# A graph layer with table casts, first gathers and node ends put in another order

## The chip, the cores and the metric

The kernel runs on one NeuronCore of a Trainium2 chip. Its engines work side by side: TensorE (PE; its weight loads are shown apart as PEld), VectorE (DVE), ScalarE (ACT), GpSimd (POOL) and SyncE (SP), which here only issues transfers. The metric is the device time of one execution in microseconds; the time of a kernel is the median of its runs.

## The reference, cut to what matters

6250 nodes with 128 features, 100000 edges sorted by destination, a message network of three layers, the mean of the messages at each destination, a node network of two layers, and a layer norm of the result:

```python
row, col = src, dst                                   # 100000 edges, dst sorted
msg_in = concatenate([x[row], x[col]], axis=-1)       # 100000 x 256
h = relu(msg_in @ Wm1 + bm1)                          # 256 wide
h = relu(h @ Wm2 + bm2)                               # 256 wide
messages = h @ Wm3 + bm3                              # 128 wide
agg = segment_sum(messages, col) / clip(count, 1)
upd = relu(concatenate([x, agg]) @ Wn1 + bn1) @ Wn2 + bn2
out = layernorm(x + (x + upd))                        # 6250 x 128
```

## The kernel before, in words

**Preparation.** The first layer is split: x @ (upper half of Wm1) is table A, x @ (lower half) is table B, both written to DRAM, one row for each node. The 49 tiles of 128 nodes are worked in 13 blocks of four (`turn` transposes, `a_table` writes A, `b_table` writes B three blocks behind). A is kept in 32 bits. B is kept as three bf16 terms: a cast of the product (L249, ACT), the rest (L250, DVE), the rest's cast (L252 on POOL for the early tiles, L254 on ACT from block 9 on), and what still remains (L255, DVE); L256 stores it (SP). The `rest` tiles have two buffers, the `bt` tiles six. `x_part` computes for a block of nodes the part of the node network that needs no messages (two products of 128x512 and a bias each); blocks 0, 1, 2 are done beside the last tables, 3 to 8 behind them, 9 and 12 inside the first two steps of the edge loop, 10 and 11 at its end.

**Edge loop.** 196 groups of 512 edges. `fetch` gathers four times 128 rows of A by source (L412, an indirect transfer on POOL; it can't start before all of A is in DRAM) and loads four windows of rows of B (L418, SP; not before all of B is in DRAM). Four `ag` and four `bw` buffers. `hot` builds one-hot matrices on DVE. `first_layer` transposes the rows of A into PSUM (L449) and adds B by a one-hot product (L455); ACT applies bias and relu (L460). `second_layer` multiplies with Wm2 (L469), DVE takes a maximum (L471). `sums` adds over destinations in a window (L478), `add_up` transposes the sums (L489) and adds them into `acc` in SBUF (L494). Groups are fetched two steps ahead; in step g PE does first layer g, sums of g - 3 and second layer g - 1. The 24 memsets that clear `acc` (L376) run on POOL.

**Node stage.** `products` (third layer of the summed messages), `hidden` (first node layer), `norm` (second node layer, the sum with 2x, statistics, square root, scale and shift, store). 15 blocks of nodes: one of 106 nodes, two of 256, ten of 512 and two of 256. `norm` runs two blocks behind `hidden`. In `norm` the tiles y, mv, sd and o have two buffers each; the scaled result o is made by ACT, one instruction for each 128 nodes (L718).

**What sets the order.** PE follows the order of the program text throughout. Elsewhere a planner orders the instructions by its own estimate of when they are ready, except inside stretches marked as manual, where an engine follows the text: DVE and ACT from the blocks 3 to 8 of `x_part` to the sixth step of the edge loop, and at the end of the edge loop. Each engine works its instructions in one queue, in order; SP's transfers, stores of A and B and loads of rows of B, share one queue too.

Of the kernel before, what the change touches and what calls it, by code (L numbers as in the profile page):

```python
# [9 lines left out]
F32 = mybir.dt.float32  # L10
# [3 lines left out]
ALU = mybir.AluOpType  # L14
# [5 lines left out]
P = 128  # L20
# [7 lines left out]
def kernel(  # L28
# [122 lines left out]
    with tc.tile_pool(name="prep", bufs=1) as prep, tc.tile_pool(  # L151
# [73 lines left out]
        INDICES = 6  # L225
        LATE = BLOCKS - 4
        xu = xT, x_sb.rearrange("p t d -> p (t d)")
# [16 lines left out]
        def b_table(t0):  # L244
            m = min(2, NT - t0)
            pbt = products(t0, m, 1)
            bt = brow.tile([P, 2 * 3 * H], BF16, name="bt").rearrange("p (t c h) -> p t c h", t=2, c=3)
            rest = brow.tile([P, 2, H], F32, name="rest", bufs=2)
            nc.scalar.copy(bt[:, :m, 0], pbt[:, :m])  # L249
            nc.vector.tensor_sub(rest[:, :m], pbt[:, :m], bt[:, :m, 0])  # L250
            if t0 < 4 * LATE:
                nc.gpsimd.tensor_copy(bt[:, :m, 1], rest[:, :m])  # L252
            else:
                nc.scalar.copy(bt[:, :m, 1], rest[:, :m])  # L254
            nc.vector.tensor_sub(bt[:, :m, 2], rest[:, :m], bt[:, :m, 1])  # L255
            nc.sync.dma_start(btab[t0 * P:(t0 + m) * P].rearrange("(t p) c h -> p t c h", p=P), bt[:, :m])  # L256
# [74 lines left out]

        X_BESIDE, X_BEHIND, X_FIRST, X_END = [0, 1, 2], [3, 4, 5, 6, 7, 8], [9, 12], [10, 11]
        assert sorted(X_BESIDE + X_BEHIND + X_FIRST + X_END) == list(range(BLOCKS))

        turn(0)
        for i in range(BLOCKS + BEHIND):
# [9 lines left out]
            if i >= BEHIND:  # L346
                for t0 in range(4 * (i - BEHIND), min(4 * (i - BEHIND) + 4, NT), 2):
                    b_table(t0)
            if BLOCKS - 1 <= i < BLOCKS - 1 + len(X_BESIDE):
                whole(x_part(X_BESIDE[i - BLOCKS + 1], bank_pb, (nc.scalar, nc.scalar)))  # L350
# [15 lines left out]

        turns = ExitStack()
        turns.enter_context(tc.manual_schedule(engines={ENG.DVE, ENG.Activation}))
        for b in X_BEHIND:
            whole(x_part(b, bank_pb, (nc.scalar, nc.vector)))  # L370


        PIECE = NPAD // 8
        for c in range(HC + 1):
            for k in range(8):
                nc.gpsimd.memset(acc[:, c, k * PIECE:(k + 1) * PIECE], 0.0)  # L376

# [17 lines left out]
    with edge, tc.tile_pool(name="wk", bufs=2) as wk, tc.tile_pool(  # L395
# [10 lines left out]

        def fetch(idx, nt, firsts):


            ag = ld.tile([P, GT, H], F32, name="ag", bufs=4)  # L410
            for j in range(GT):
                nc.gpsimd.indirect_dma_start(  # L412
                    out=ag[:, j, :], out_offset=None, in_=atab[:, :],
                    in_offset=bass.IndirectOffsetOnAxis(ap=idx[:, j:j + 1], axis=0))
            bw = ld.tile([P, 2, H], BF16, name="bw", bufs=4)
# [116 lines left out]
        for i in range(NG + ahead + 1):  # L532
# [11 lines left out]
            if i < NG:  # L544
# [4 lines left out]
                elif i % 2 == 0:  # L549
                    dbs = early.pop(0) if early else destinations(i, min(2, NGF - i), dst_row)  # L550
                st[i] = dict(nt=nt, got=fetch(srcT[:, i, :], nt, firsts), db=dbs.pop(0))
            g = i - ahead
# [17 lines left out]
            if 0 <= g < NG:  # L570
                s = st[g]
                s["h1"] = first_layer(ag, bw, oht, s["nt"])
                if first:

                    make_hot(g + 1)
                    whole(x_part(first.pop(0), bank_p2, (nc.scalar, nc.vector)))
            k = g - lag
            if 0 <= k < NG:
                s = st[k]
                s["part"] = sums(s["oh"], s["h2"], s["nt"])  # L580
            m = g - 1
            if 0 <= m < NG:
                s = st[m]
# [61 lines left out]
    with tc.tile_pool(name="nd", bufs=2) as nd, tc.tile_pool(name="nr", bufs=1) as nr, tc.tile_pool(  # L645
# [43 lines left out]

        def norm(b, u):  # L690
            n0, n1 = nodes_of[b]
# [9 lines left out]
            nc.sync.dma_start(x2[:r, :k], x2tab[n0:n1, :].rearrange("(t p) d -> p t d", p=r))  # L701
            y = nd.tile([P, 4, D], F32, name="y")
            nc.vector.tensor_add(y[:r, :k, :], x2[:r, :k, :], pot[:r, :k, :])  # L703
            st = nd.tile([P, 4, 6], F32, name="st")
            mv = nd.tile([P, 4, 2], F32, name="mv")
            for i in range(k):
                nc.vector.bn_stats(st[:r, i, :], y[:r, i, :])
                nc.vector.bn_aggr(mv[:r, i, :], st[:r, i, :])
            sd = nd.tile([P, 4], F32, name="sd")
            nc.scalar.activation(sd[:r, :k], mv[:r, :k, 1], AF.Sqrt, bias=eps[:r])  # L710
            rs = nd.tile([P, 4], F32, name="rs")
            nc.vector.reciprocal(rs[:r, :k], sd[:r, :k])  # L712
            sh = nd.tile([P, 4], F32, name="sh")
            nc.vector.scalar_tensor_tensor(sh[:r, :k], mv[:r, :k, 0], -1.0, rs[:r, :k],  # L714
                                           op0=ALU.mult, op1=ALU.mult)
            o = nd.tile([P, 4, D], F32, name="o")
            for i in range(k):
                nc.scalar.activation(o[:r, i, :], y[:r, i, :], AF.Identity, bias=sh[:r, i:i + 1],  # L718
                                     scale=rs[:r, i:i + 1])
            if r == P:  # L720
# [7 lines left out]
        us = {}  # L728
        for b in range(B + BACK):
            if b < B:  # L730
                us[b] = hidden(b, aggs.pop(b))
            if b >= BACK:
                norm(b - BACK, us.pop(b - BACK))
            if b + FORE < B:
                aggs[b + FORE] = products(b + FORE)


# [27 lines left out]
```

## Time and profile before

| What | us |
|---|---|
| median of 4 runs | 1210.07 (1208.21 to 1212.18) |
| profiled execution, its own time | 1207.48 |
| its span, first to last instruction | 1205.7 |
| PE busy | 1176.4 |
| POOL busy | 804.4, of which 784 gathers 752.6 |
| DVE, ACT busy | 670.8, 454.8 |
| PE starts on the first group of edges | 82.89 |
| last gather ends | 1098.3 |
| node stage's first product on PE | 1130.1 |
| PE's last product ends | 1195.96 |
| ACT's last instruction ends | 1202.78 |

Times in the timelines count from the start of the span. A line of a timeline has the start, the length (from the start of the first to the end of the last of a merged run), the engine, the line of the kernel, the operation, output and inputs, the number of instructions, and in brackets how long the engine had been idle before it and what ended that. PE and the weight loads overlap, and matmuls are pipelined, so a busy PE is not a PE at its peak. The granted TensorE clock is 0.998 of full speed over the span.

### The profile page before, as it was taken

The page shows a single profiled execution, that of the slowest core. Times are in us where ns is not written, and L with a number is a line of the kernel's source. Part 1 is how long each engine was busy: PE and PEld are TensorE (multiplying, and loading weights), DVE is VectorE, ACT ScalarE, POOL GpSimd, SP SyncE. Part 2 cuts the span into 40 slices and gives each one's busy share as a digit, 9 for nine tenths or more (in the row PEclk, how much of TensorE's full clock was granted, in tenths as well). Part 3 has the DMA queues.
Part 4 walks back from the last instruction along what each step waited for, and adds up shares of the span by engine and source line. Part 5 has one row for each costly group of instructions (what it writes and reads, how often), then busy time and mean ns, then how long its engine had stood idle before and what let it go on. Part 6 is the DMA issues. An engine that isn't in the chain of part 4 may idle for free. (4 is left out here: it accounts for less than half of the span.)

```text
span 1205.7 us, 32797 instructions
## 1 busy us (share of the span) xinstructions
PE 1176.4 (98%) x11196; PEld 893.8 (74%) x11197; DVE 670.8 (56%) x2080; ACT 454.8 (38%) x1163; POOL 804.4 (67%) x859
## 2 busy tenths in 40 slices
PE   7989999999999999999999999999999999999996
PEld 6747777777777777777777777777777777777565
DVE  5863655555555555555555555555555555555586
ACT  5663333333333333333333333333333333333256
POOL 8267777777777777777777777777777777773220
PEclk9999999999999999999999999999999999999999
DMA  9886666666555555555555555555555555552333
GB/s 294 289 258 180 184 183 178 191 188 181 152 152 148 151 149 153 154 152 152 151 147 150 153 153 152 148 155 148 149 153 153 152 152 151 145 150 62 96 111 105
DMA packets 173672, 193.66 MB, mean 161 GB/s; under 512 B 30844, under 2 KB 145486, under 8 KB 173488
## 3 DMA queue, kind: packets, MB, share of 16 engines
q0 software_dynamic: 37984, 103.35, 31.1%
q1 hardware_dynamic: 106956, 61.93, 17.7%
q10 hardware_dynamic: 28564, 26.27, 8.2%
q8 instruction: 90, 1.47, 0.5%
q14 instruction: 78, 0.64, 0.2%
HBM read 168.92 MB, written 22.88 MB: 159 GB/s over the span
## 5 line engine op out<-in xcount | busy, mean ns | idle before, releaser
L412 POOL DMA_INDIRECT ag<-atab,srcT x784 | 752.6, 960 | 282.5 <-issue 184.6
L469 PE MATMUL ph<-w,h 128*128 128x256 f32 x3128 | 727.5, 386 | 1.2 <-ACT x_sb L318 1.2
L469 PEld LDWEIGHTS ph<-w,h 128*128 128x128 f32 x3128 | 578.1, 190 | 152.4 <-DVE acc L494 65.7
L460 ACT ACTIVATE h<-ph,b 128x256 f32<-128x256 f32 x782 | 307.1, 475 | 674.9 <-PE ph L455 505.4
L471 DVE TENSOR_TENSOR h<-ph,nb 128x512 f32<-128x512 f32 x391 | 270.4, 692 | 412.8 <-PE ph L469 409.0
L494 DVE TENSOR_TENSOR acc<-acc,pt 128x63 f32 x782 | 172.2, 220 | 33.5 <-PE ph L455 2.9
L449 PE MATMUL ph<-ident,ag 64*128 64x64 f32 x3128 | 129.9, 223 | 0.6 <-DVE b L382 0.6
L478 PE MATMUL pg<-h,oh 128*32 128x257 f32 x1564 | 125.6, 392 | 0.0
L449 PEld LDWEIGHTS ph<-ident,ag 64*128 64x128 f32 x3128 | 113.2, 139 | 2.1 <-ACT h L460 0.8
L433 DVE TENSOR_SCALAR oht<-db,pbase 128x128 bf16<-128x128 int32 x392 | 105.5, 344 | 1.2 <-PE ph L455 1.0
L489 PEld LDWEIGHTS pt<-ident,part 64*128 64x128 f32 x1173 | 51.1, 136 | 66.4 <-issue 65.8
L455 PE MATMUL ph<-oht,bw 64*128 64x128 bf16 x1564 | 76.8, 216 | 3.0 <-DMA bw<-btab 2.6
L489 PE MATMUL pt<-ident,part 64*128 64x64 f32 x1173 | 78.0, 238 | 0.6 <-DVE acc L494 0.4
L481 ACT COPY part<-pg 128x257 f32<-128x257 f32 x196 | 76.8, 392 | 4.0 <-PE pg L478 4.0
L436 DVE TENSOR_TENSOR oh<-iota_n,dloc 128x128 f32<-128x128 f32 x196 | 55.1, 281 | 21.3 <-PE pg L478 20.2
L676 POOL TENSOR_TENSOR agg<-total,rc 128x512 f32<-128x512 f32 (+2 forms) x15 | 16.0, 1070 | 69.1 <-DVE total L673 62.1
L455 PEld LDWEIGHTS <-bw 64*128 64x128 bf16 x1564 | 53.5, 96 | 3.8 <-DMA bw<-btab 3.2
L232 PE MATMUL pbt<-w,xT 128*128 128x256 f32 x196 | 48.1, 391 | 2.4 <-ACT bt L241 1.2
L478 PEld LDWEIGHTS pg<-h,oh 128*32 128x32 f32 x1564 | 30.8, 108 | 21.7 <-issue 0.8
L232 PEld LDWEIGHTS pbt<-w,xT 128*128 128x128 f32 x196 | 36.5, 195 | 10.7 <-ACT bt L241 2.4
L252 POOL CAST bt<-rest 128x512 bf16<-128x512 f32 x18 | 11.9, 664 | 26.3 <-DVE rest L250 17.2
L698 PEld LDWEIGHTS pot<-wu,u 128*128 128x128 f32 (+1 forms) x196 | 24.0, 191 | 5.5 <-issue 4.8
(109 smaller groups left out, 416.5 us busy)
## 6 DMA issues: line engine op xcount, KB each, us to landing
bw<-btab SPq DMA_DIRECT2D x782, 32.0 KB
db<-in_dst_dram ACTq DMA_DIRECT2D x194, 128.0 KB
ag<-atab,srcT POOLq DMA_INDIRECT x784
btab<-bt SPq DMA_DIRECT2D x24, 384.0 KB
atab<-bt SPq DMA_DIRECT2D x24, 256.0 KB
xd<-in_x_dram SPq DMA_DIRECT2D x12, 256.0 KB
x2tab<-xd SPq DMA_DIRECT2D x12, 256.0 KB
x_sb<-in_x_dram SPq DMA_DIRECT2D x5, 512.0 KB
```

The source lines that it names most:

```text
L232: nc.tensor.matmul(pbt[:, a, :], xT[:, (t0 + a) * P:(t0 + a + 1) * P], w1[:, k, :], start=True, stop=True)
L412: nc.gpsimd.indirect_dma_start(out=ag[:, j, :], out_offset=None, in_=atab[:, :], in_offset=bass.IndirectOffsetOnAxis(ap=idx[:, j:j + 1], a ...
L433: nc.vector.tensor_scalar(oht[:n, k, :], db[:n, k * P:(k + 1) * P], pb_cols[:n, k:k + 1], None, op0=ALU.is_equal)
L449: nc.tensor.matmul(phs[h][:, c, u * NQ:(u + 1) * NQ], ag[halves[h], u, c * P:(c + 1) * P], ident[halves[h], halves[h]], is_transpose=True, ...
L455: nc.tensor.matmul(phs[h][:, c, k * P:(k + 1) * P], bw[halves[h], k, c * P:(c + 1) * P], oht[halves[h], k, :], start=False, stop=True, ski ...
L460: nc.scalar.activation(h1[:, c, h * 2 * P:(h + 1) * 2 * P], phs[h][:, c, :], AF.Relu, bias=b1[:, c:c + 1])
L469: nc.tensor.matmul(ph2[:, a, :], h1[:, c, (j0 + a) * P:(j0 + a + 1) * P], w2[:, c, :], start=(c == 0), stop=(c == HC - 1))
L471: nc.vector.tensor_tensor(h2[:, j0:j0 + 2, :H], ph2, nb2.to_broadcast([P, 2, H]), op=ALU.max)
L478: nc.tensor.matmul(pg[j * WN:(j + 1) * WN, :], oh[:, j, :], h2[:, j, :], start=True, stop=True, skip_group_check=True)
L481: nc.scalar.copy(part[:n, :], pg[:n, :])
L489: nc.tensor.matmul(pt[:, c, :], rows, ident[halves[h], halves[h]], is_transpose=True, start=True, stop=True, skip_group_check=True)
L494: nc.vector.tensor_add(window, window, pts[j // 2][:, :, k:k + WB])
```

## The change

- The second term of B is always cast on POOL; the cast on ACT for the late tiles goes.
- The memsets of `acc` come first, and from there to the sixth step of the edge loop POOL too follows the order of the text.
- The gathers of the first two columns of group 0 are put after the tables of blocks 10 and 11, so that the casts of the last blocks lie between and behind them; the other two follow in `fetch`.
- Before the gathers of groups 3, 4 and 5, DVE copies one element of the first layer's result of group 0, 1 and 2 into the `ag` tile, so that the gather can't start before that result is there.
- `x_part`: blocks 0 and 1 beside the tables, 2 to 7 behind, 8 in the first step of the loop, 9 and 12 in the second, there with the first half's bias on DVE and the second's on ACT (before: the other way round).
- Second layer 0 is done in step 0, behind block 8, not in step 1.
- `norm` is split into `moments`, `deviation` and `scaled`. y, mv, sd and o get three buffers. For the last three blocks DVE and ACT follow the text, the scaling of a block stands behind the moments of the next, and some of its 128-node pieces are done on DVE.

```diff
-            if t0 < 4 * LATE:
-                nc.gpsimd.tensor_copy(bt[:, :m, 1], rest[:, :m])
-            else:
-                nc.scalar.copy(bt[:, :m, 1], rest[:, :m])
+            nc.gpsimd.tensor_copy(bt[:, :m, 1], rest[:, :m])
...
-        X_BESIDE, X_BEHIND, X_FIRST, X_END = [0, 1, 2], [3, 4, 5, 6, 7, 8], [9, 12], [10, 11]
+        X_BESIDE, X_BEHIND, X_FIRST, X_END = [0, 1], [2, 3, 4, 5, 6, 7], [[8], [9, 12]], [10, 11]
...
+        PIECE = NPAD // 8
+        for c in range(HC + 1):
+            for k in range(8):
+                nc.gpsimd.memset(acc[:, c, k * PIECE:(k + 1) * PIECE], 0.0)
+        turns = ExitStack()
+        turns.enter_context(tc.manual_schedule(engines={ENG.Pool}))
+
+        def gather(ag, idx, js):
+            for j in js:
+                nc.gpsimd.indirect_dma_start(
+                    out=ag[:, j, :], out_offset=None, in_=atab[:, :],
+                    in_offset=bass.IndirectOffsetOnAxis(ap=idx[:, j:j + 1], axis=0))
+
+        def rows_of_a():
+            return ld.tile([P, GT, H], F32, name="ag", bufs=4)
+
+        first_rows = rows_of_a()
         turn(0)
         for i in range(BLOCKS + BEHIND):
...
             if i >= BEHIND:
                 for t0 in range(4 * (i - BEHIND), min(4 * (i - BEHIND) + 4, NT), 2):
                     b_table(t0)
+            if i - BLOCKS in (0, 1):
+                gather(first_rows, srcT[:, 0, :], [i - BLOCKS])
             if BLOCKS - 1 <= i < BLOCKS - 1 + len(X_BESIDE):
                 whole(x_part(X_BESIDE[i - BLOCKS + 1], bank_pb, (nc.scalar, nc.scalar)))
...
-        def fetch(idx, nt, firsts):
-            ag = ld.tile([P, GT, H], F32, name="ag", bufs=4)
-            for j in range(GT):
-                nc.gpsimd.indirect_dma_start(
-                    out=ag[:, j, :], out_offset=None, in_=atab[:, :],
-                    in_offset=bass.IndirectOffsetOnAxis(ap=idx[:, j:j + 1], axis=0))
+        def fetch(idx, nt, firsts, rows=None, have=(), gate=None):
+            ag = rows or rows_of_a()
+            if gate is not None:
+                nc.vector.tensor_copy(ag[0:1, 0, 0:1], gate)
+            gather(ag, idx, [j for j in range(GT) if j not in have])
...
-                st[i] = dict(nt=nt, got=fetch(srcT[:, i, :], nt, firsts), db=dbs.pop(0))
+                more = dict(rows=first_rows, have=(0, 1)) if i == 0 else {}
+                if 3 <= i <= 5:
+                    more["gate"] = st[i - 3]["h1"][0:1, 0, 0:1]
+                st[i] = dict(nt=nt, got=fetch(srcT[:, i, :], nt, firsts, **more), db=dbs.pop(0))
...
                     make_hot(g + 1)
-                    whole(x_part(first.pop(0), bank_p2, (nc.scalar, nc.vector)))
+                    for b in first.pop(0):
+                        whole(x_part(b, bank_p2, (nc.vector, nc.scalar)))
...
-            m = g - 1
-            if 0 <= m < NG:
+            m = g - 1 if g else g
+            if 0 <= m < NG and "h2" not in st[m]:
...
-            y = nd.tile([P, 4, D], F32, name="y")
+            y = nd.tile([P, 4, D], F32, name="y", bufs=3)
...
+        for b in range(B - 1):
+            us[b] = hidden(b, aggs.pop(b))
             if b >= BACK:
-                norm(b - BACK, us.pop(b - BACK))
+                y, mv = moments(b - BACK, us.pop(b - BACK))
+                scaled(b - BACK, y, mv, deviation(b - BACK, mv), [nc.scalar] * 4)
             if b + FORE < B:
                 aggs[b + FORE] = products(b + FORE)
+        with tc.manual_schedule(engines={ENG.DVE, ENG.Activation}):
+            us[B - 1] = hidden(B - 1, aggs.pop(B - 1))
+            ends = [(B - 3, [nc.scalar, nc.scalar, nc.scalar, nc.vector]), (B - 2, [nc.scalar, nc.vector]),
+                    (B - 1, [nc.vector, nc.scalar])]
+            before = None
+            for b, engines in ends:
+                y, mv = moments(b, us.pop(b))
+                sd = deviation(b, mv)
+                if before:
+                    scaled(*before)
+                before = b, y, mv, sd, engines
+            scaled(*before)
```

In `scaled` a piece on ACT is the activation as before (identity with scale and bias by node); on DVE it is a `tensor_scalar` of 128x128, multiply and add, with the same two columns.

More of the change, by code (lines that the diff above doesn't have):

```diff
@@ L225 @@
         INDICES = 6
-        LATE = BLOCKS - 4
         xu = xT, x_sb.rearrange("p t d -> p (t d)")
@@ L328, in bank_pb @@
             return pb.tile([P, 2, H], F32, name="pxu", tag="pbt")
-        X_BESIDE, X_BEHIND, X_FIRST, X_END = [0, 1, 2], [3, 4, 5, 6, 7, 8], [9, 12], [10, 11]
-        assert sorted(X_BESIDE + X_BEHIND + X_FIRST + X_END) == list(range(BLOCKS))
+        X_BESIDE, X_BEHIND, X_FIRST, X_END = [0, 1], [2, 3, 4, 5, 6, 7], [[8], [9, 12]], [10, 11]
+        assert sorted(X_BESIDE + X_BEHIND + sum(X_FIRST, []) + X_END) == list(range(BLOCKS))
+        PIECE = NPAD // 8
[12 more added lines that the diff above has]
+        first_rows = rows_of_a()
         turn(0)
@@ L365 @@
         early = [destinations(2 * k, 2, dst_row) for k in range(3)]
-        turns = ExitStack()
         turns.enter_context(tc.manual_schedule(engines={ENG.DVE, ENG.Activation}))
@@ L370 @@
             whole(x_part(b, bank_pb, (nc.scalar, nc.vector)))
[L373 to L376, printed above, removed]
         pb3 = pp.tile([P, 1], F32, name="pb3", tag="pp")
@@ L688, in hidden, with moments @@
             return u
-        def norm(b, u):
+        def moments(b, u):
             n0, n1 = nodes_of[b]
@@ L701, in norm @@
             nc.sync.dma_start(x2[:r, :k], x2tab[n0:n1, :].rearrange("(t p) d -> p t d", p=r))
-            y = nd.tile([P, 4, D], F32, name="y")
+            y = nd.tile([P, 4, D], F32, name="y", bufs=3)
             nc.vector.tensor_add(y[:r, :k, :], x2[:r, :k, :], pot[:r, :k, :])
             st = nd.tile([P, 4, 6], F32, name="st")
-            mv = nd.tile([P, 4, 2], F32, name="mv")
+            mv = nd.tile([P, 4, 2], F32, name="mv", bufs=3)
             for i in range(k):
@@ L708, in norm, with deviation, scaled @@
                 nc.vector.bn_aggr(mv[:r, i, :], st[:r, i, :])
-            sd = nd.tile([P, 4], F32, name="sd")
-            nc.scalar.activation(sd[:r, :k], mv[:r, :k, 1], AF.Sqrt, bias=eps[:r])
+            return y, mv
+        def deviation(b, mv):
+            r = min(P, nodes_of[b][1] - nodes_of[b][0])
+            k = -(-(nodes_of[b][1] - nodes_of[b][0]) // P)
+            sd = nd.tile([P, 4], F32, name="sd", bufs=3)
+            nc.scalar.activation(sd[:r, :k], mv[:r, :k, 1], AF.Sqrt, bias=eps[:r])
+            return sd
+        def scaled(b, y, mv, sd, engines):
+            n0, n1 = nodes_of[b]
+            k = -(-(n1 - n0) // P)
+            r = min(P, n1 - n0)
             rs = nd.tile([P, 4], F32, name="rs")
@@ L715, in norm @@
                                            op0=ALU.mult, op1=ALU.mult)
[L716 to L719, printed above, removed]
+            o = nd.tile([P, 4, D], F32, name="o", bufs=3)
+            for i, eng in zip(range(k), engines):
+                if eng is nc.scalar:
+                    eng.activation(o[:r, i, :], y[:r, i, :], AF.Identity, bias=sh[:r, i:i + 1], scale=rs[:r, i:i + 1])
+                else:
+                    eng.tensor_scalar(o[:r, i, :], y[:r, i, :], rs[:r, i:i + 1], sh[:r, i:i + 1],
+                                      op0=ALU.mult, op1=ALU.add)
             if r == P:
@@ L728 @@
         us = {}
-        for b in range(B + BACK):
-            if b < B:
-                us[b] = hidden(b, aggs.pop(b))
+        for b in range(B - 1):
+            us[b] = hidden(b, aggs.pop(b))
             if b >= BACK:
-                norm(b - BACK, us.pop(b - BACK))
+                y, mv = moments(b - BACK, us.pop(b - BACK))
+                scaled(b - BACK, y, mv, deviation(b - BACK, mv), [nc.scalar] * 4)
             if b + FORE < B:
                 aggs[b + FORE] = products(b + FORE)
+        assert BACK == 2
+        with tc.manual_schedule(engines={ENG.DVE, ENG.Activation}):
[10 more added lines that the diff above has]
+            scaled(*before)
 _INS = ['x', 'src', 'dst', 'L0_gnn_Wm1', 'L0_gnn_bm1', 'L0_gnn_Wm2', 'L0_gnn_bm2', 'L0_gnn_Wm3',
```

## The prediction

> **What bounds the kernel now.** I read the page first (share of each engine, the 40 slices), then the table of groups, then the waits of PE alone, and last the timelines of the only two places where PE is not full: the passage into the edge loop (60 to 105 us) and the end (1190 us on).
>
> ```profile
> PE 1176.4 (98%) x11196; PEld 893.8 (74%) x11197; DVE 670.8 (56%) x2080; ACT 454.8 (38%) x1163; POOL 804.4 (67%) x859
> PE   7989999999999999999999999999999999999996
> L412 POOL DMA_INDIRECT ag<-atab,srcT x784 | 752.6, 960 | 282.5 <-issue 184.6
> ```
>
> PE is the bound: 29 us of the 1205.7 are idle, at both ends of the span. In the loop a group repeats each 5.27 us on PE (the part transposes start at 111.09 and again at 116.36), while its four gathers take 4 x (0.96 + 0.30) = 5.04 us on POOL. So POOL follows PE by a hair, which matters for anything that starts the gathers later. The passage, on PE:
>
> ```profile
> 82.89 0.71 PE L449 MATMUL ph<-ident,ag 64*128 64x64 f32 x16 [0.57 <-DVE b L382]
> 84.76 0.23 PE L455 MATMUL ph<-oht,bw 64*128 64x128 bf16 x2 [1.07 <-DMA bw<-btab]
> 85.45 0.34 PE L455 MATMUL ph<-oht,bw 64*128 64x128 bf16 x5 [0.46 <-DMA bw<-btab]
> 89.09 0.23 PE L455 MATMUL ph<-oht,bw 64*128 64x128 bf16 x2 [0.69 <-DMA bw<-btab]
> 89.73 0.34 PE L455 MATMUL ph<-oht,bw 64*128 64x128 bf16 x5 [0.40 <-DMA bw<-btab]
> 91.92 3.72 PE L469 MATMUL ph<-w,h 128*128 128x256 f32 x16 [1.23 <-ACT x_sb L318]
> ...
> 96.44 3.72 PE L469 MATMUL ph<-w,h 128*128 128x256 f32 x16
> ```
>
> The reader is to see 4.4 us of waiting: 2.6 for rows of B, 1.2 for a PSUM bank that ScalarE frees late, 0.6 at the change of pools. Behind 96.44 PE waits 0.3 and 0.4 us once each and then not again until the node stage. The rows of B are late because table B is:
>
> ```profile
> 76.59 0.39 ACT L254 CAST bt<-rest 128x256 bf16<-128x256 f32 x1
> 77.02 0.43 DVE L255 TENSOR_TENSOR bt<-rest,bt 128x256 bf16<-128x256 f32 x1 [0.64 <-ACT bt L254]
> 77.47 0.34 SPq L256 DMA_DIRECT2D btab<-bt  x1
> 81.09 0.57 SPq L418 DMA_DIRECT2D bw<-btab  x1
> ```
>
> The last cast of B sits behind work of the node parts on ScalarE, the last store goes out at 77.47, and the first load of its rows can be issued only at 81.09, 3.6 us later. The end, on VectorE and ScalarE:
>
> ```profile
> 1194.05 0.69 DVE L703 TENSOR_TENSOR y<-x,pot 128x512 f32<-128x512 f32 x1 [0.56 <-ACT o L718]
> 1196.89 0.42 DVE L703 TENSOR_TENSOR y<-x,pot 128x256 f32<-128x256 f32 x1 [0.83 <-ACT o L718]
> 1199.47 0.42 DVE L703 TENSOR_TENSOR y<-x,pot 128x256 f32<-128x256 f32 x1 [1.34 <-ACT o L718]
> ```
>
> PE ends at 1195.96, ScalarE at 1202.78. Each y waits until ScalarE has read the y two blocks before (two buffers): 2.7 us in three waits, one after another.
>
> **The change part by part, against the profiled execution of 1207.48 us** (span 1205.7; it is 2.6 below the median 1210.07, as runs here scatter from 1208.21 to 1212.18). Differences carry over to the median.
>
> **Casts.** Seven casts leave ScalarE (six of 0.62, one of 0.39) for POOL, whose 18 casts have a median of 0.61. No time is saved in the instruction; what goes is the place in ScalarE's queue. The rest tiles have two buffers, so the chain is cast, third term, next rest. In the before the last two pairs went: rests done 72.69, casts from 73.16 to 74.28, third terms to 75.39, last rest 75.30, cast 76.59, third term to 77.45. With a block of the node parts (1.72 us of PE) less ahead of it, the last product of B leaves PE at about 69.7 in place of 71.4, and a pair costs VectorE 4 x 0.65 = 2.6 us, as it did at 61.12 to 64.3 with POOL's casts, without holes. From 67.0 the pairs then end at 69.7 and 72.4, the single tile at 73.6, the store goes at 73.7. If up to three bias additions of the node parts (0.65 each) are put between, 75.7. I take 74.7, 2.8 earlier.
>
> ```profile
> L252 POOL CAST bt<-rest x18: 601/613/1153, 24.7 to 62.6; 128x512 bf16<-128x512 f32 x18
> L254 ACT CAST bt<-rest x7: 394/621/629, 65.7 to 76.6; 128x512 bf16<-128x512 f32 x6, 128x256 bf16<-128x256 f32 x1
> ```
>
> The columns are minimum, median and maximum in ns: POOL's longest is 1153. The third terms read two SBUF operands on VectorE at that moment. [...]
>
> **Two gathers among the casts.** 1.26 us each on POOL, ahead of the casts of the last two blocks. They wait for table A, which had landed at 65.77 (POOL's first gather); they are reached at about 68.7, so they don't wait. They can hold a cast by 0 to 1.26 us; the single tile's rest is ready at 72.5 by the above, gather two ends at about 73.0, so 0.5, inside the 2 us left for the store.
>
> **Fewer gathers early.** In the before ten were issued by 78 us, while the DMA engines were 81 to 100% busy (70 to 80 us, five windows of 2 us). Now two by then, and the other two of the first group right behind. So a store lands no later than its 3.6 us; at best after the 2.2 us that a last gather of the loop took from its end (1098.3) to DMA silence. I take 3.6: first load at 78.3, and the fourth used 4.36 later as before (81.09 to 85.45): 82.7.
>
> **PE's passage.** First layer 0 starts at 82.89 - 1.72 = 81.2 (the 0.57 stays). Then 0.87 work, 0.7 wait for rows of B, block 8 1.72, 0.15 for a bank, second layer 0 3.5, first layer 1 0.87, blocks 9 and 12 2.15, 0.45 since block 12's second bank hangs on ScalarE behind four relus (1.57), first layer 2 0.87: 92.4 where the before has 96.44. Gain 4.0. The rows of B for first layer 1 have 5.2 us more, so their 1.09 goes. Bounds: no wait at all gives 5.0; table B not a bit earlier gives 1.0; gathers late (below) take up to 1.5 off. I take 3.7, range -0.5 to 5.
>
> **POOL's start.** POOL has issued 9 gathers by 77.5 in the before, now about 3. From 73.6: group 0 complete at 76, groups 1 to 4 at 81, 86, 91, 96.4; plus 2.2 to land. PE wants group 1 at 88, 2 at 91.6, 3 at 96, 4 at 101. Two to five us to spare, growing by 0.23 a group: cost 0, bound 0 to 1.5 if POOL starts as late as ScalarE's last cast now (77).
>
> **Gates.** Three one-element copies on VectorE (nearest row 0.14, 128x1 copies into db) hold groups 3, 4, 5 until relu of 0, 1, 2 (84, 90, 94). VectorE runs in written order there: the gate of group 5 sits behind second layer 1's maxima, 96.4, just when POOL arrives. POOL queues behind each; the one-hot of group 3 queues behind the last gate on VectorE: 0.1 on a wait that is 0.3 today. Cost 0 to 0.3, taken 0.1.
>
> **Memsets** of the sums first on POOL: 24 of 0.75 from 7.24 end at 25.3; the first cast was at 24.72. 0.6 later, not on PE's path (0 to 0.6). Engines swapped in the node parts: nothing beyond the banks above.
>
> **End.** Three buffers for y, mv, sd, o, and VectorE and ScalarE in written order. VectorE's own work from 1190.94: 0.61 and 1.3 for block 11, additions 0.66, reciprocal and shift 0.3, then y and statistics 1.8, 1.0, 1.0, three reciprocals and shifts 0.8, three rows of o at 0.2 (nearest: a 128x128 tensor_scalar, L433, 0.28 with its overlap) 0.6: 8.1, to 1199.1; waits for ScalarE's root, 0.5 to 1.2. Last o about 1200.1 where it is 1202.78. Gain 2.7; 3.7 without any wait, 0 if the written order makes block 11's o hold the last relus (0.6) and the roots. The store of the result (2.9 from there to the span's end) stays.
>
> **Sum:** 3.7 + 2.7 - 0.1 = 6.3: profiled 1201.2, median 1203.8.
>
> **The rivals.** (1) The passage gains nothing: POOL becomes its bound, casts wait behind gathers, or first groups land late. For: 5.04 against 5.27. Against: two us to spare. Only the end gains: 1207.4. (2) The end gains nothing, the written order trading one wait for another; for: ScalarE's 482 ns per row of o, VectorE nearly full there. Only the passage: 1206.5. (3) Slower: in the steady loop VectorE's order is left to the planner, and a shifted start can give another order for 190 groups. One place shows the price: first layer 3 waits 0.33 us for a one-hot queued behind a maximum. At 0.035 us a group the whole gain is eaten; at 0.1 it is 1222. For: PE has no slack. Against: VectorE is 56% busy and the loop's text is unchanged.
>
> **How the numbers follow.** Forecast 0.63 (1200.8 to 1206), rival 1 0.13, rival 2 0.10, rival 3 0.12, anything else 0.02. 0.2%, 2.4 us, is what a measurement of this kernel can tell. Faster: the forecast, rival 2, half of rival 1: 0.79. Same: the rest of rival 1, a little of the others: 0.09. Slower 0.12. The range goes from all best bounds but one (1200.8) past rival 1 to 1208.6.
>
> **What would show it.** Right: last store of B before 76, first load of rows before 79.5; PE's waits for rows of B under 1 us; second layer 1 at 92 to 93.5; no wait of PE for ag; in the end no y waiting for o, ScalarE done 5 us or less after PE. Wrong: PE waiting for ag, a period above 5.27 us, or a third term waiting for POOL by microseconds.

## The result: 2.2 us faster, and the profile after

| | before | after |
|---|---|---|
| median | 1210.19 us of 56 runs (1207.73 to 1213.41) | 1208.03 us of 35 runs (1204.16 to 1210.49) |
| ratio | | 0.9982, 95% interval 0.9977 to 0.9987 |
| profiled execution, span | 1207.48, 1205.7 | 1207.72, 1206.0 |
| granted clock over that span | 0.998 | 0.995 |

The forecast was 1203.8. The sign and the range held; the gain is 2.2 us where 6.3 were forecast. The two profiled executions take the same time, so the difference has to be read in stretches. I cut both traces, and later those of the experiments, at four marks on PE: the start of the fifth group of transposes in the preparation, of second layer 1 (the mark that the prediction used), of the node stage's first product, and of the last product of `hidden` (L685 before, L701 after).

| stretch, us | before | after | difference |
|---|---|---|---|
| start to fifth transposes | 16.91 | 18.87 | +1.96 |
| to second layer 1 ("passage") | 79.53 | 80.19 | +0.66 |
| to the node stage ("loop") | 1033.62 | 1032.70 | -0.92 |
| to the last product of `hidden` ("node stage") | 60.63 | 61.23 | +0.60 |
| to the end of the span ("end") | 15.0 | 13.0 | -2.0 |
| span | 1205.7 | 1206.0 | +0.3 |

The first stretch, in which the work is nearly the same, is set aside: in the traces of the experiments the first mark lies between 16.8 and 18.0 us, whatever the kernel. Only the end moved as forecast. The passage, which was to bring 3.7, lost 0.66 in this trace. The timeline of PE in the profile of after (start, length, engine, line, operation, count, and in brackets the idle time ahead and its releaser):

```profile
75.14 7.99 PE L312 MATMUL pxu<-xT,wu 128*128 128x512 f32 x18 [0.78 <-ACT x_sb L314]
82.97 0.50 PE L392 MATMUL pb<-b,w 128*128 128x1 f32 x4
84.04 0.71 PE L459 MATMUL ph<-ident,ag 64*128 64x64 f32 x16 [0.57 <-DVE b L393]
84.74 0.21 PE L465 MATMUL ph<-oht,bw 64*128 64x128 bf16 x1
85.74 0.23 PE L465 MATMUL ph<-oht,bw 64*128 64x128 bf16 x2 [0.79 <-DMA bw<-btab]
86.88 0.35 PE L465 MATMUL ph<-oht,bw 64*128 64x128 bf16 x5 [0.91 <-DMA bw<-btab]
87.17 3.62 PE L312 MATMUL ph<-xT,wu 128*128 128x512 f32 x4
90.62 3.62 PE L479 MATMUL ph<-w,h 128*128 128x256 f32 x16
...
97.80 0.47 PE L312 MATMUL ph<-xT,wu 128*128 128x106 f32 x2 [0.32 <-ACT xT L314]
...
99.06 3.72 PE L479 MATMUL ph<-w,h 128*128 128x256 f32 x16
```

The new order is there: block 8 and second layer 0 follow first layer 0, and the waits for rows of B at the second first layer and the 1.23 for ScalarE's bank are gone. But block 8, four matmul instructions of 128x512, took 3.62 us; in before's trace such four (there block 9) took 1.98:

```profile
85.72 1.98 PE L316 MATMUL ph<-xT,wu 128*128 128x512 f32 x4
```

The windows of two us of after say why (columns: window, its length, busy time and instructions of PE, PEld, DVE, ACT, POOL, then the granted clock, the DMA share, GB/s):

```profile
84.00:86.00 2.00, 1.14 (x19) 0.76 (x19) 1.58 (x12) 0.00 (x0) 1.56 (x2) 1.00 0.65 170
86.00:88.00 2.00, 1.12 (x6) 0.67 (x7) 0.00 (x0) 0.66 (x2) 1.53 (x2) 0.77 0.70 189
88.00:90.00 2.00, 2.00 (x4) 0.67 (x2) 0.72 (x1) 0.91 (x3) 1.39 (x3) 0.50 0.94 217
90.00:92.00 2.00, 2.00 (x9) 1.51 (x8) 0.03 (x1) 0.69 (x1) 0.91 (x1) 0.88 0.65 172
```

Behind the waits of PE between 83.5 and 86.9 the granted clock falls to half, at about 87.1, and stays there until about 90.5. In before's profiled execution the clock is 1.00 in each window from 84 to 98, though PE is idle there for longer (3.5 us of these 14, in after 2.1); one of its windows:

```profile
86.00:88.00 2.00, 2.00 (x15) 0.76 (x15) 0.20 (x1) 2.00 (x5) 1.39 (x3) 1.00 0.99 245
```

The node stage of after shows it again: its first 16 products (L687) took 5.71 us where before's took 4.16, at a clock of 0.50 from 1132 to 1134; both had waited 2.3 us just ahead. Before, then after:

```profile
1130.06 4.16 PE L671 MATMUL pmt<-acc,w 128*128 128x106 f32 x16 [2.30 <-DVE rc L665]
```

```profile
1131.76 5.71 PE L687 MATMUL pmt<-acc,w 128*128 128x106 f32 x16 [2.32 <-DVE rc L681]
```

So the question for the runs was whether the clock ate the passage's gain, and whether before pays the same in other executions than the one I had read.

The table of B, in the profile of after, on VectorE and GpSimd by time:

```profile
70.94 1.81 POOL L250 CAST bt<-rest 128x512 bf16<-128x512 f32 x2 [1.39 <-DVE rest L249]
...
75.75 1.25 POOL L343 DMA_INDIRECT ag<-atab,srcT  x1 [0.17 <-issue]
...
77.85 0.40 POOL L250 CAST bt<-rest 128x256 bf16<-128x256 f32 x1 [0.85 <-issue]
```

```profile
72.79 0.69 DVE L251 TENSOR_TENSOR bt<-rest,bt 128x512 bf16<-128x512 f32 x1 [0.51 <-POOL bt L250]
...
75.06 1.07 DVE L251 TENSOR_TENSOR bt<-rest,bt 128x512 bf16<-128x512 f32 x1 [0.38 <-POOL bt L250]
76.06 0.74 DVE L316 TENSOR_SCALAR xT<-pxu,bu 128x512 f32<-128x512 f32 x1
76.72 0.68 DVE L251 TENSOR_TENSOR bt<-rest,bt 128x512 bf16<-128x512 f32 x1
...
77.65 0.74 DVE L316 TENSOR_SCALAR xT<-pxu,bu 128x512 f32<-128x512 f32 x1
78.31 0.41 DVE L251 TENSOR_TENSOR bt<-rest,bt 128x256 bf16<-128x256 f32 x1
```

Two casts that follow each other take 1.81, not 1.22, and a third term beside a cast takes 1.07, not 0.69: where a cast and a third term run side by side, one of the two takes longer. The last third term ends at 78.7 and not at 74.7; the first rows of B are asked for at 82.02 and not at 78.3. And the end, VectorE in after:

```profile
1195.84 0.69 DVE L720 TENSOR_TENSOR y<-x,pot 128x512 f32<-128x512 f32 x1
1196.55 0.18 DVE L741 RECIPROCAL rs<-sd 128x4 f32<-128x4 f32 x1
1196.65 0.26 DVE L724 BATCH_NORM_STATS2 st<-y 128x6 f32<-128x128 f32 x1
1196.83 0.15 DVE L743 SCALAR_TENSOR_TENSOR sh<-mv,rs 128x4 f32<-128x4 f32 x1
1196.94 0.18 DVE L725 BATCH_NORM_AGGREGATE mv<-st 128x2 f32<-128x6 f32 x1
1197.04 0.26 DVE L724 BATCH_NORM_STATS2 st<-y 128x6 f32<-128x128 f32 x1
...
1198.23 0.40 DVE L720 TENSOR_TENSOR y<-x,pot 128x256 f32<-128x256 f32 x1
```

No y waits for an o any more. But from y to y the block of four pieces takes 2.39 us, since in the written order each aggregate stands right behind its statistics, about 0.40 for each pair of the two.

### The profile page after: what moved, and what is told of

Same layout as the page of the kernel before. It is cut to its first block, busy times and chain, and to the rows that moved or that the text cites. A ratio compares the mean times of both kernels' runs of the same rounds, so it can differ in the third digit from the quotient of the medians.

```text
span 1206.0 us, 32823 instructions
## 1 busy us (share of the span) xinstructions
PE 1180.9 (98%) x11196; PEld 896.2 (74%) x11197; DVE 675.4 (56%) x2087; ACT 450.1 (37%) x1152; POOL 811.1 (67%) x866
## 5 line engine op out<-in xcount | busy, mean ns | idle before, releaser
L499 PEld LDWEIGHTS pt<-ident,part 64*128 64x128 f32 x1173 | 50.8, 136 | 65.6 <-issue 65.2
L250 POOL CAST bt<-rest 128x512 bf16<-128x512 f32 (+1 forms) x25 | 16.9, 684 | 33.2 <-DVE rest L249 19.8
```

Of the source, the lines that this page charges most:

```text
L499: nc.tensor.matmul(pt[:, c, :], rows, ident[halves[h], halves[h]], is_transpose=True, start=True, stop=True, skip_group_check=True)
```

## The experiments

In the expectations the theories go by letters. The two that carried the study: A, that the node end is all of the median's gain and the passage brings nothing; C, that the passage's gain goes into the granted clock. Edits are against the kernel after the change, where nothing else is said.

### The same kernels where every group waits

The first four kernels and the last two ran on chips on which the kernel before takes 1452.69 and 1429.81 us. There PE waits for 0.6 us on the mean in the middle of first layers, in 201 to 265 places, for nothing that the profile shows; the waits of PE in the profile of the kernel before with the new end (line, waited for, total, times, longest):

```profile
PE ph L455 <- issue: 140.7, 253, 1.3
```

In the traces from the chips on which before takes 1210 us that line is 0.4 us at most, in one wait. So the times from there can't be put beside the others, and an expectation that was stated for 1210 us is not answered by them. Four kernels:

Only the end changed (before with after's node stage from `hidden` on):

```diff
-        def norm(b, u):
+        def moments(b, u):
...
+        with tc.manual_schedule(engines={ENG.DVE, ENG.Activation}):
+            us[B - 1] = hidden(B - 1, aggs.pop(B - 1))
```

> The kernel before with only the new node end (three buffers, written order, pieces of o on VectorE); tables, passage and loop stay. Theory A (the end gives 2.0 us, as the two traces show when they are laid on each other at the last first-layer product of the node stage: 1190.69 to 1205.7 before, 1192.99 to 1206.0 after): 2.0 us faster than before, and the rest of the change is worth nearly nothing in the median. Rival B (the end gives nothing in the median and the gain of 2.2 us comes from the passage): within 0.5 us of before.

Measured: 1450.26, ratio 0.9985 (0.9973 to 0.9996): 2.2 us faster, close to the 2.0 of theory A.

All but the end changed:

```diff
-        def moments(b, u):
+        def norm(b, u):
...
-            y = nd.tile([P, 4, D], F32, name="y", bufs=3)
+            y = nd.tile([P, 4, D], F32, name="y")
...
-        for b in range(B - 1):
-            us[b] = hidden(b, aggs.pop(b))
+        for b in range(B + BACK):
+            if b < B:
+                us[b] = hidden(b, aggs.pop(b))
```

> The changed kernel with the node end of before. Theory A: within 0.5 us of before, since the passage gives back what it gains. Rival B: 2 us or more faster than before. In the trace the passage should again show PE waiting for rows of B; if the granted clock falls to half behind that wait in this execution too, the drop belongs to the passage and isn't an accident of one profile.

Measured: 1466.47, ratio 1.0089 (1.0073 to 1.0104), 13 us slower, which neither theory had.

Block 8 of `x_part` in front of first layer 0, so that PE has work while the rows of B are on their way:

```diff
-        X_BESIDE, X_BEHIND, X_FIRST, X_END = [0, 1], [2, 3, 4, 5, 6, 7], [[8], [9, 12]], [10, 11]
+        X_BESIDE, X_BEHIND, X_FIRST, X_END = [0, 1], [2, 3, 4, 5, 6, 7, 8], [[9], [12]], [10, 11]
```

> The changed kernel with block 8 of the node parts done ahead of first layer 0 and block 9 alone in step 0, block 12 in step 1: the same work on PE, 1.72 us of it moved into the time in which PE waits for rows of B. Theory C (in the changed kernel PE's idle time at the passage, 0.6 + 0.8 + 0.9 us within 3 us, makes the granted clock fall to half for some 4 us, which costs about 2 us on top of the waits): the wait shrinks from 1.7 to under 0.5, the clock stays at 1.00 at 84 to 92 us, and the time is 1.5 to 3.5 us below the changed kernel's, about 1205. Rival D (the clock does not depend on that wait): only the wait shrinks, 1.0 to 1.5 us below the changed kernel, clock rows below 1.00 as before. Rival E (first layer 0 then waits for the same load at a later place): no gain.

Measured: 1462.5, ratio 1.0068 (1.0054 to 1.0082).

Statistics of all pieces of a block first, then all aggregates, in `moments`:

```diff
             for i in range(k):
                 nc.vector.bn_stats(st[:r, i, :], y[:r, i, :])
+            for i in range(k):
                 nc.vector.bn_aggr(mv[:r, i, :], st[:r, i, :])
```

> The changed kernel with the statistics of all pieces of a block ahead of their aggregations, in place of each aggregation right behind its statistics. Theory F (in written order each aggregation waits for the statistics just ahead: a pair takes 0.40 us where the planner's interleaved order takes 0.30, ten pairs on the path of the end): 0.6 to 1.0 us faster than the changed kernel, the y of the last block about 0.6 earlier against PE's end. Rival G (the end waits for ScalarE's root and scale, not for VectorE): no change within 0.3 us.

Measured: 1461.52, ratio 1.006 (1.0044 to 1.0076). The last two were run once more, to tell what each of the two edits brings by itself, and met the other such chip:

> Block 8 ahead of first layer 0, node end as in the changed kernel; on a chip where the kernel before takes 1210 us. Theory C (the granted clock falls at the passage because TensorE waits there, and that is where the passage's gain went): the clock stays at 1.00 from 80 to 98 us, second layer 1 starts 77.5 to 79.5 us after the turn of the first products, and the time is 1205.2 to 1206.5 us, ratio 0.9955 to 0.997. Rival N (the gain of the variant with both edits lay in the node end alone): the passage gains nothing over the changed kernel's, 1207.5 to 1208.5 us, ratio 0.998.

Measured: 1440.48, ratio 1.007 (1.0058 to 1.0082).

> The passage of the changed kernel, statistics and aggregates in two loops; on a chip where the kernel before takes 1210 us. Theory C: the clock falls at the passage as in the changed kernel, the node end takes 12.0 us behind the last put in place of 13.0, and the time is 1206.7 to 1207.5 us, ratio 0.997 to 0.9978. Rival N (the gain of the variant with both edits lay in the node end alone): 1204.5 to 1205.2 us, ratio 0.9955.

Measured: 1437.8, ratio 1.0053 (1.0039 to 1.0067). Neither theory C nor its rival gave a number for such a chip, and neither is told by these two runs.

What follows: on such a chip all that has the new passage is slower than before, by 0.5 to 0.9%, and the new end alone is 0.15% faster. The end itself does there what it does elsewhere: from the last product of `hidden` to the end of the span it takes 15.1 us in all but the end, 13.0 in the new end alone and in both traces of block 8 in front, and 12.0 in both with the statistics apart. The loss lies at the start of the loop. The windows of the new end alone, and then of all but the new end, on the same chip:

```profile
110.00:160.00 50.00, 43.13 (x406) 31.75 (x401) 21.76 (x73) 14.07 (x39) 28.98 (x30) 0.97 0.56 147
200.00:1200.00 1000.00, 861.72 (x8304) 638.44 (x8306) 423.15 (x1388) 280.16 (x765) 589.40 (x614) 1.00 0.47 127
```

```profile
110.00:160.00 50.00, 35.78 (x309) 25.59 (x310) 17.02 (x57) 12.66 (x34) 28.91 (x31) 0.83 0.50 133
200.00:1200.00 1000.00, 860.32 (x8309) 638.61 (x8308) 423.59 (x1392) 281.29 (x769) 590.02 (x615) 1.00 0.47 127
```

From 200 us on the loops run alike (861.7 and 860.3 us of PE work in 1000); between 110 and 160 the kernel with the new passage does 97 matmuls fewer, at a mean granted clock of 0.83 against 0.97, and PE stands once for 6.0 us, up to 113.8, until ScalarE has done the activation of a first layer (h). What holds it there was not found.

### All but the end, again, at 1210 us

> The changed kernel with the node end of before, once more, since the first run of it fell on a chip where the kernel before took 1453 us. On a chip that runs the kernel before in about 1210 us: theory A (the end is all of the gain in the median) within 0.5 us of before; rival B (the passage gains) 1 to 2 us faster. If the granted clock falls to half at 86 to 92 us here too, the drop belongs to this passage.

Measured: 1210.15 where before took 1209.6; ratio 1.0003 (0.9994 to 1.0012). So theory A stands: casts, gathers, gates and the new passage together brought nothing in the median, to within about 1 us. Its end is 15.0 us, as before's. Its trace has the clock's fall three times: in the preparation, from 60 to 63 us; 0.73 and 0.50 in the windows 86 to 90; and at the node stage, where the first 16 products took 7.27 us. The first of these lies in the stretch called passage, and after's trace does not have it. All but the end, then after:

```profile
60.00:70.00 10.00, 10.00 (x33) 7.03 (x32) 6.96 (x11) 7.14 (x14) 3.87 (x6) 0.85 0.82 291
```

```profile
60.00:70.00 10.00, 9.54 (x34) 6.28 (x35) 7.53 (x12) 7.37 (x15) 5.11 (x6) 1.00 0.92 328
```

### Work in place of the waits, and the statistics apart

Both edits, block 8 in front and statistics ahead of aggregates.

> The changed kernel with two edits whose places lie apart, so that one trace shows both: block 8 of the node parts ahead of first layer 0 (block 9 alone in step 0, block 12 in step 1), and at the end the statistics of all pieces of a block ahead of their aggregations. On a chip that runs the kernel before in about 1210 us: theory C (PE's idle time at the passage drops the granted clock to half) expects the clock at 1.00 from 84 to 92 us and second layer 1 about 3 us earlier against the same starting point (99.06 - 18.87 = 80.2 us after the turn at 18.87 in the changed kernel); rival D (the clock does not hang on that wait) 1.0 to 1.5 earlier. Theory F (text order of statistics and aggregation costs 0.1 us a pair) expects the end 0.6 to 1.0 us shorter from the last put of the node stage (13.0 us in the changed kernel, 15.0 before). Together 1204 to 1205.5, 2 to 4 us below the changed kernel.

Measured: 1204.67 (1203.76 to 1205.18), ratio 0.9956 (0.9942 to 0.9969). The profile of that kernel, PE:

```profile
84.30 0.72 PE L459 MATMUL ph<-ident,ag 64*128 64x64 f32 x16 [0.57 <-DVE b L393]
...
85.55 0.34 PE L465 MATMUL ph<-oht,bw 64*128 64x128 bf16 x5 [0.18 <-issue]
85.81 1.98 PE L312 MATMUL ph<-xT,wu 128*128 128x512 f32 x4
```

No wait for rows of B, the four matmuls behind first layer 0 (here block 9's) in 1.98 again, and the clock is 1.00 in every window from 84 to 98. The passage takes 77.61 us, 2.6 less than after's, where theory C had about 3 and its rival 1.0 to 1.5, and the end 12.0 in place of 13.0, with the statistics run together:

```profile
1194.07 0.87 DVE L724 BATCH_NORM_STATS2 st<-y 128x6 f32<-128x128 f32 x4
1194.85 0.36 DVE L726 BATCH_NORM_AGGREGATE mv<-st 128x2 f32<-128x6 f32 x4
```

That is 1.14 us from the first statistics to the end of the aggregates' run, where after's four pairs took 1.66 (1196.65 to 1198.31). But in two of the next groups PE waits for rows of A (0.59 at 99.59, 0.79 and 0.19 at 111.06 and 111.53; 1.6 us together). They are late because POOL stood before a gate, a copy that VectorE reaches only at 92.22, behind second layer 0's maxima; the profile puts the wait down to the one-hot that VectorE had just ended:

```profile
92.62 1.16 POOL L343 DMA_INDIRECT ag<-atab,srcT  x1 [3.03 <-DVE oht L443]
```

### Work that nobody reads

Two more products of 128x512 (four matmul instructions), into PSUM banks that nothing reads, just ahead of the place where PE waits. All that the kernel computes stays.

```diff
+        for c in range(HC):
+            idle = bank_pb().rearrange("p t h -> p (t h)")
+            nc.tensor.matmul(idle, wu1[:, 0, c * P:(c + 1) * P], xT[:, N - 4 * P:N], start=True, stop=True)
```

> The changed kernel with 1.72 us of work added that nobody reads: two more products of 128x512 behind blocks 2 to 7, ahead of first layer 0; all that the kernel computes stays. Theory C (PE's waits at the passage drop the granted clock to half for about 4 us, which costs about 2 us more): the added work lies in the wait for rows of B, the clock stays at 1.00 at 84 to 92 us, second layer 1 starts 1 to 2 us earlier against the same turn (80.2 to 81.2 us after the fifth turn in the two traces with the drop), and the time falls by 1 to 2 us below the changed kernel's although it does more. Rival D (the clock doesn't hang on the wait): unchanged or up to 1 us slower.

Measured: 1206.17, ratio 0.9966 (0.9953 to 0.9979), against 0.9982 (0.9977 to 0.9987) for after: more work, and less time by about 1.9 us, though these are 5 runs and the two intervals just touch. In its trace the added work (L390) takes 1.9 us, the waits for rows of B shrink to 0.50, and the clock stays up:

```profile
82.44 1.88 PE L390 MATMUL pxu<-xT,wu 128*128 128x512 f32 x4
...
86.27 0.34 PE L468 MATMUL ph<-oht,bw 64*128 64x128 bf16 x5 [0.50 <-DMA bw<-btab]
86.53 1.98 PE L312 MATMUL ph<-xT,wu 128*128 128x512 f32 x4
88.59 3.69 PE L482 MATMUL ph<-w,h 128*128 128x256 f32 x16
```

```profile
86.00:88.00 2.00, 1.73 (x9) 0.84 (x9) 0.59 (x3) 0.77 (x3) 1.55 (x2) 1.00 0.62 158
88.00:90.00 2.00, 1.92 (x9) 1.28 (x8) 0.45 (x1) 1.38 (x4) 1.54 (x2) 1.00 0.72 205
```

Nothing was taken out of the work, no order was changed, and the table of B came no earlier (first load of its rows 63.5 us after the first mark, after: 63.15). Counted from the first mark, block 8 starts at 68.50 here and at 68.30 in after, and second layer 1 starts at 79.08 here and at 80.19 there: the start is 0.2 later, and block 8 at the full clock is 1.4 shorter. So in these two traces the difference is the clock. The passage also scatters from one execution to the next (79.53 and 83.20 in before), so the medians, and not this one pair of traces, have to say what it is worth.

### The same without gates

```diff
-                if 3 <= i <= 5:
+                if False:
```

on top of both edits above.

> fill_split without the three gates: no copies of an element into the gathers' tiles of groups 3, 4, 5. In the trace of fill_split PE waits 1.6 us for gathered rows (three waits), behind a 3.0 us pause of POOL. Theory H (the gates now cost what they hold back): those waits go to under 0.3 us, time 1.0 to 1.6 us below fill_split's, about 0.9945 of before. Rival I (the gathers that are let go collide with the loads of rows of B, and PE waits for those in their place): no gain, waits for rows of B of 1 us or more.

Measured: 1202.51 (1201.34 to 1203.72), ratio 0.9932 (0.992 to 0.9945). PE's waits for rows of A are gone, and none for rows of B came in their place. It is the fastest kernel of the study, 8.0 us below before's median there, 1210.51. How much of the last step is the gates is not settled: it ran on another chip than the kernel with gates, and in the two traces the way from the first mark to the node stage is 1111.7 with gates and 1111.8 without.

### The late casts back on ScalarE

```diff
-            nc.gpsimd.tensor_copy(bt[:, :m, 1], rest[:, :m])
+            if t0 < 4 * (BLOCKS - 4):
+                nc.gpsimd.tensor_copy(bt[:, :m, 1], rest[:, :m])
+            else:
+                nc.scalar.copy(bt[:, :m, 1], rest[:, :m])
```

> The changed kernel with the seven late casts of B on ScalarE again, all else as changed. Theory J (a cast on POOL and a third term on VectorE take turns, as the pair of 1.81 us and the 0.51 us waits of the third terms in the changed kernel's trace show, so that a pair of tiles takes 3.2 us on VectorE in place of 2.6 and the last store comes late): the last store of B 1 to 2 us earlier against the same turn (59.9 us after the fifth turn in the changed kernel, 60.6 before), first load of rows of B earlier by the same, time 0.5 to 2 us below the changed kernel's. Rival K (ScalarE is as late, as in the kernel before): last store the same or later, no gain.

Measured: 1208.66, ratio 0.9988 (0.998 to 0.9997). The guess (theory J) that GpSimd's casts hold table B back, and that ScalarE's would bring it sooner, fell, and its rival K held: the first rows of B are asked for 65.2 us after the first mark, and PE waits 2.6 us for them. In the five traces with these casts on GpSimd they are asked for after 63.2 to 64.9 us (63.15 in after, with a wait of 1.7). The stretched third terms do end; those on VectorE in this profile:

```profile
71.81 1.29 DVE L254 TENSOR_TENSOR bt<-rest,bt 128x512 bf16<-128x512 f32 x2 [1.07 <-ACT bt L253]
...
75.33 1.29 DVE L254 TENSOR_TENSOR bt<-rest,bt 128x512 bf16<-128x512 f32 x2 [0.37 <-ACT bt L253]
```

Two of them take 1.29, none of the late ones takes 1.07. So the stretch goes with the casts on GpSimd, and ending it brought the table no sooner. In time the two places of the casts are not told apart (0.9988 and 0.9982, with intervals that overlap).

### Before, looked at again

The kernel before, unchanged, in order to see another execution of it.

> The kernel before once more, for a second trace of it: its first trace had a mean granted clock of 0.998, and the runs listed beside fill_split have 0.992 to 0.995. Theory C: the trace shows the clock at half at 86 to 96 us here too, so the execution that the prediction was made on was one without the drop and 2 to 3 us faster than most. Rival L: no drop in this stretch; the clock is lost elsewhere.

Measured: 1210.59 against 1210.51; ratio 1.0 (0.999 to 1.001). Its profiled execution (span 1211.2) has the clock's fall that the first one lacked; PE, and the windows that go with it:

```profile
93.44 6.70 PE L469 MATMUL ph<-w,h 128*128 128x256 f32 x16 [1.23 <-ACT x_sb L318]
```

```profile
92.00:94.00 2.00, 0.77 (x3) 0.53 (x3) 0.33 (x1) 1.38 (x5) 1.70 (x2) 0.67 0.52 136
94.00:96.00 2.00, 2.00 (x6) 1.62 (x5) 0.00 (x0) 0.00 (x0) 1.39 (x3) 0.50 0.51 156
96.00:98.00 2.00, 2.00 (x6) 1.55 (x6) 0.69 (x1) 0.00 (x0) 1.67 (x2) 0.50 0.56 161
```

Second layer 0 takes 6.70 us where the first trace had 3.72; the passage is 83.20 where it was 79.53. Each timed execution lists its mean granted clock over the span: of 23 of before on this chip, 20 are at 0.994 or less and one at 0.998, the figure of the profiled execution that I had read. In that profile all that is missing lies behind 1200 us, where PE has ended; so the lower figures most likely mean a fall somewhere earlier, but they don't say where. Nor do they order before's times: the one at 0.998 took 1209.91, near the median. The execution that I had read, at 1207.48, lies below all 56 timed runs.

### All in one table

| kernel | passage | loop | node stage | end | median | ratio |
|---|---|---|---|---|---|---|
| before, first trace | 79.53 | 1033.62 | 60.63 | 15.0 | 1210.19 | 1 |
| before, second trace | 83.20 | 1034.63 | 60.63 | 15.0 | 1210.59 | 1.0 |
| after | 80.19 | 1032.70 | 61.23 | 13.0 | 1208.03 | 0.9982 |
| all but the end | 81.20 | 1033.89 | 62.79 | 15.0 | 1210.15 | 1.0003 |
| late casts on ScalarE | 82.34 | 1033.59 | 60.63 | 13.0 | 1208.66 | 0.9988 |
| work nobody reads | 79.08 | 1033.01 | 61.37 | 12.9 | 1206.17 | 0.9966 |
| block 8 in front, statistics apart | 77.61 | 1034.12 | 61.34 | 12.0 | 1204.67 | 0.9956 |
| the same without gates | 79.21 | 1032.61 | 61.25 | 12.1 | 1202.51 | 0.9932 |

The stretches are those of one trace each; the medians are of 5 and more runs. The ends agree to 0.1 us wherever the code is the same, the loop scatters by two, and the passage by up to 3.7 (before).

## Why the prediction was wrong, point by point

**End, 2.7: right, mis-sized.** 2.0 by the traces: 15.0 in the three with the old end, 12.9 to 13.0 in the three with the new one. In the median it is after's 0.9982 against 1.0003 for all but the end, 0.0021 of 1210, 2.5 us. I had costed y and its statistics for four pieces at 1.8; it took 2.39. Where the planner had set two statistics side by side, the written order has statistics and aggregate in turn. Taking them apart gave 1.0 more (12.0): 3.0 in all, where my bound without any wait was 3.7.

**Passage, 3.7: the step that failed, and with it the sum.** By terms, in after's trace, with after's start set back by the 1.96 that it lost before the first mark:

| step of the prediction | forecast | measured |
|---|---|---|
| start of first layer 0 | 81.2 | 82.08 |
| first layer 0 with the wait for rows of B | 1.57 | 3.13 |
| block 8 and a bank | 1.87 | 3.45 |
| second layer 0 | 3.5 | 3.55 |
| first layer 1 | 0.87 | 0.86 |
| blocks 9 and 12 with the wait for a bank | 2.6 | 3.17 |
| first layer 2 | 0.87 | 0.86 |
| second layer 1 | 92.5 | 97.10 |

The largest single error, 1.58, is block 8 at the half clock: no term of the sum had a price for the clock. The next, 1.56, is the wait for rows of B, 0.7 forecast and 1.70 measured, and the work about it, 0.87 forecast and 1.43 measured; before's own first layer 0 has 1.30 of work (82.89 to 85.72, less 1.53 of waits). The 0.9 at the start is a bank that ScalarE frees late (0.78 at 75.14). The last, 0.57, is the work of blocks 9 and 12: I had 2.15, and they take 2.6 in before's trace. Together the rows make 4.6 us. Without the clock's 1.6 there would still be 3.0 of mis-sized terms, and about 0.9 would be left of the 3.7.

**"Differences carry over to the median": a second step that failed.** The execution that I read was one in which PE waited 4.4 us in the passage and lost no clock. Most others of the same kernel list a lower clock, and the one other trace of it lost 3.0 us behind nearly the same waits, so differences against the first trace are not differences against the median. All but the end has a ratio of 1.0003: in the median the passage brought nothing. How much before loses to the clock in the median, and in which stretch, is not shown. For after, the executions listed with a clock of 0.993 or 0.994 took 1209.0 on the mean of 17, those at 0.996 or 0.997 took 1206.9 on the mean of 13: 2.1 us apart, about what the run with useless work gained. But the listed clock holds every fall of the span, the one at the node stage too, so this is no measure of the passage alone. The fall of the clock is shown for the passage, and that work in place of the waits ends it; why it comes in one execution of a kernel and not in the next is not.

**Casts: mis-sized.** They came off ScalarE's queue, but the rows of B could be asked for only 1.0 us sooner (63.15 us after the first mark, 64.18 in before's first trace), where 2.8 was forecast, and in before's second trace and among the other traces with the new casts the figure goes up to 64.9, so even the 1.0 is within the scatter. I had 2.6 us for a pair on VectorE and named 61.12 to 64.3 of before for it; that stretch is 3.1 us long, since its two third terms took 1.75 together and not 1.3:

```profile
62.58 1.75 DVE L255 TENSOR_TENSOR bt<-rest,bt 128x512 bf16<-128x512 f32 x2
```

Its two rows are 1.15 and 0.68 long. In after a pair took 3.2 to 3.3. Casts and third terms ran side by side at each pair of the last blocks, and the cast (up to 1.16 for 0.61) or the third term (1.07 for 0.69) was stretched; the sum has no term for that. Two bias additions of 0.74 between the last terms did the rest.

**Two gathers among the casts, 0.5 at most.** The second one ended at 77.0 and not at 73.0, and the last cast, at 77.85, follows it by 0.85 us and had no need to wait for it: its rest ended at 77.7. The first, from 72.92 to 74.40, held a cast by 0.3 at most, since that cast's rest ended at 74.08.

**POOL's start: right.** PE waited for no gather in after. **Gates: the time was wrong, the price right for after.** Group 3's gate came at 94.88 behind second layer 0's maxima, not at 84, and POOL stood for 4.38 us. That cost PE nothing in after, because PE was late; with the passage mended PE waited 1.6 us behind it. **Memsets and swapped engines:** no wait of PE shows them.

**The rivals.** Rival 1, the passage gains nothing and the median is 1207.4, is what happened (1208.03), but not by its mechanism: neither gathers nor POOL held the passage. Rival 2 fell, since the end gained. Rival 3, a worse order in the steady loop, fell on these chips: the period is still 5.27 us and the loop of after is the shortest but one of the table. On the chips on which before takes 1430 and 1453 us the changed passage is the slower one, by a mechanism that I had not thought of and did not find.

## What to carry to other kernels

Where PE is the bound, a cluster of waits can cost more than its length: price it with the half clock behind it (here 1.4 to 3.0 us for a fall in the passage), and try to fill it, even with work that nobody reads, before moving anything else. Look at the granted clock of the execution that you build a sum on, and at that of the timed ones; if it is the best of all, its stretches are not the median's. Two instructions on VectorE and GpSimd that were never seen side by side have no price in their own medians: look at their longest rows (in before 1.15 us for both, against medians of 0.61 and 0.69).

## What the runs showed of the hardware that was not expected

- In after's trace the clock fell to half behind waits of 0.57, 0.79 and 0.91 us between 83.5 and 86.9. Four matmul instructions then took 3.62 us for 1.98, and with work in the waits the median was about 2 us lower. Before's two traces show that such waits don't always bring it: PE waited 4.4 us in the one and 4.5 in the other between 82 and 94 us, and the clock was at 1.00 throughout in the one and at 0.50 for 94 to 98 in the other. What decides it, no run here shows.
- The clock fell again at the node stage in the five traces of kernels with the new casts, but not in before's two nor in the one with the late casts on ScalarE (60.63 us each, against 61.2 to 62.8); a wait of 2.3 us stands ahead of that place in all eight. No run was made on it.
- A cast on GpSimd and a third term on VectorE that run side by side: the cast's 0.61 becomes 1.16 or the third term's 0.69 becomes 1.07. One of the two is stretched, by 0.55 or 0.38 us in after (a third term by up to 0.45 in before), and the other keeps its time.
- The same kernel took 1210 us on some chips and 1430 to 1453 on others, where the long matmuls take as long in the steady loop (the 16 of a second layer 3.72 us, at 602.83 in the new end alone on such a chip and at 603.90 in before) and PE has waits that no record explains (140.7 us in 253 places in the new end alone); there the order of the variants was another.
